# Transposed operands of a two-layer graph network: rearranging DMAs and 32x32 VectorE transposes with an HBM scratch, in place of TensorE transposes

## The chip, the cores and the metric

The kernel runs on one core of one Trainium2 chip. The metric is the device time of one execution in microseconds (us), on that core. "Clock" is the mean TensorE clock that the throttle granted, as a share of full speed. On one core there is no second die to compare with. The sessions ran on different chips; each ratio is to the kernel before in the same rounds on the same chip.

## The reference, cut to what matters

Batch 32, 512 nodes, 512 features, all fp32. Two layers, each with a LayerNorm without weights, a relu and a residual:

```python
h = max(layernorm(x), 0)
agg = (adj @ h) / max(rowsum(adj), 1e-6)
x = x + relu(concat(h, agg) @ W.T)                 # layer 0

h = max(layernorm(x), 0)
q, k = split(h @ Wqk);  v = h @ Wv
w = mask * rowdot(q, adj @ (mask * k)) / sqrt(512)
x = x + softmax(w, over nodes)[:, None] * v        # layer 1
```

Both kernels fold the weights so that one batch has five products of 512x512 matrices: y = h·W2, z = h·W1 + adj'·y (two products in one accumulator), q = h1·(Wq Wkᵀ), g = adj'·h1, and v = h1·Wv. adj' is the adjacency divided by the degree; layer 1 multiplies w by the degree again. A 512x512 product is done by Strassen's scheme in its Winograd form: seven half-size products of sums of quarters instead of eight.

The products here sum over the partitions of both operands. The left operands h (hT), h1 (h1T) and adj' (aT) must therefore be there transposed. The change is about how that happens.

## The kernel before

Each left operand is transposed by TensorE in 128x128 blocks into PSUM, the memory that TensorE writes its results to, and ScalarE evicts (copies out) four blocks at a time:

```python
def transpose_rows(dst, src, c, name):
    p = ps_t.tile([P, 2, 2, P], F32, tag="t", name=name)
    for d in range(4):
        nc.tensor.transpose(p[:, d // 2, d % 2, :], src(d), ident)
    half, m = divmod(c, 2)
    nc.scalar.activation(dst[:, 2 * half:2 * half + 2, :, ts(m, P)], p, AF.Copy)

def prepare(b):
    h0 = tile4(big, "h0", 1, f"h0_{b}")
    layer_norm(b, f"0_{b}", lambda c: h0[:, c, :])
    HT[b] = operand(big, "hT", 1, f"hT_{b}")
    for c in range(C):
        transpose_rows(HT[b], lambda d: h0[:, c, ts(d, P)], c, f"pth_{b}_{c}")
    left_sums(nc.vector, HT[b])
    # ... degree by a row sum, adjacency scaled by 1/degree on ScalarE ...
    for c in range(C):
        transpose_rows(AT[b], lambda d: an[:, c, ts(d, P)], c, f"pta_{b}_{c}")
    left_sums(nc.gpsimd, AT[b])
```

A product evicts three partial sums (r1, u2, u3) with ScalarE and ends its quarters on VectorE (mostly an add, and for z and v a "finish" into x). In the profiles, u3v is the sum u3 of product v, and av, bv and cv are v's three PSUM banks. The sixth of the seven groups of a product can't start before u3 is evicted, because it goes into the same PSUM bank. The batches are laid over one another in this order:

```python
for i in range(B):
    layer0_out(i)                # z of batch i
    if i > 0:
        layer1_out(i - 1)        # v of the batch before, output written
    if i + 1 < B:
        prepare(i + 1)           # LayerNorm 0's result and adjacency, transposed
        layer0_y(i + 1)          # y of the next batch
    layer1_h(i)                  # LayerNorm 1, h1T
    layer1_w(i)                  # q, g, softmax weights
    # ... cut: load(i + 2)
```

A scheduler fixes the order of every engine's queue at compile time, by its own estimate of when each instruction will be ready. An instruction that was written earlier may therefore come out later.

Of the kernel before, what the change touches and what calls it, by code (L numbers as in the profile page):

```python
# [10 lines left out]
F32 = mybir.dt.float32  # L11
# [4 lines left out]
P = 128  # L16
H = 256
# [5 lines left out]
def kernel(  # L23
# [23 lines left out]

    nc = tc.nc
# [9 lines left out]
    small = ctx.enter_context(tc.tile_pool(name="small", bufs=3))  # L58
    ps_t = ctx.enter_context(tc.tile_pool(name="ps_t", bufs=2, space=bass.MemoryType.PSUM))
# [26 lines left out]
    X, A = {}, {}  # L86

    def load(b):
        X[b] = tile4(big, "x", 3, f"x_{b}")
        nc.sync.dma_start(out=X[b], in_=x[b].rearrange("(c p) f -> p c f", p=P))  # L90
        A[b] = tile4(big, "adj", 1, f"adj_{b}")
        nc.sync.dma_start(out=A[b], in_=adj[b].rearrange("(c p) j -> p c j", p=P))

    def transpose_rows(dst, src, c, name):

        p = ps_t.tile([P, 2, 2, P], F32, tag="t", name=name)
        for d in range(4):
            nc.tensor.transpose(p[:, d // 2, d % 2, :], src(d), ident)  # L98
        half, m = divmod(c, 2)
        nc.scalar.activation(dst[:, 2 * half:2 * half + 2, :, ts(m, P)], p, AF.Copy)  # L100
# [55 lines left out]
    mask_sb = const.tile([B, N], F32, name="mask_sb")  # L156
    nc.sync.dma_start(out=mask_sb, in_=nodemask)
    w_in = []
    for half, tag in ((w0[:, F:2 * F], "x"), (w0[:, 0:F], "x"), (wqk[:, 0:F], "q"), (wqk[:, F:2 * F], "aT")):
        t = tile4(big, tag, {"x": 3, "q": 1, "aT": 2}[tag], f"w_in{len(w_in)}")  # L160
        nc.sync.dma_start(out=t, in_=half.rearrange("(c p) f -> p c f", p=P))
        w_in.append(t)
    w1, w2, wm, wvv = (operand(const, n, 1, n) for n in ("w1", "w2", "wm", "wvv"))
    for d in range(D):
        kh, kt = divmod(d, 2)
        nc.sync.dma_start(
            out=wvv[:, 2 * kh:2 * kh + 2, kt, :], in_=wv[ts(d, P), :].rearrange("p (n f) -> p n f", n=2)
        )
# [4 lines left out]
    HT, AT, Y, DEG = {}, {}, {}, {}  # L173
# [16 lines left out]
    def prepare(b):  # L190
        h0 = tile4(big, "h0", 1, f"h0_{b}")
        layer_norm(b, f"0_{b}", lambda c: h0[:, c, :])
        HT[b] = operand(big, "hT", 1, f"hT_{b}")
        for c in range(C):
            transpose_rows(HT[b], lambda d: h0[:, c, ts(d, P)], c, f"pth_{b}_{c}")
        left_sums(nc.vector, HT[b])

        deg = small.tile([P, C], F32, tag="deg", name=f"deg_{b}")
        rdeg = small.tile([P, C], F32, tag="rdeg", name=f"rdeg_{b}")
        nc.vector.tensor_reduce(deg, A[b], AX.X, ALU.add)  # L200
        nc.vector.tensor_scalar(deg, deg, DEG_EPS, None, op0=ALU.max)
        nc.vector.reciprocal(rdeg, deg)
        DEG[b] = deg
        an = A.pop(b)
        for c in range(C):
            nc.scalar.activation(an[:, c, :], an[:, c, :], AF.Copy, scale=rdeg[:, c:c + 1])
        AT[b] = operand(big, "aT", 2, f"aT_{b}")
        for c in range(C):
            transpose_rows(AT[b], lambda d: an[:, c, ts(d, P)], c, f"pta_{b}_{c}")
        left_sums(nc.gpsimd, AT[b])  # L210
# [21 lines left out]
    def layer1_h(b):  # L232

        h1 = H1[b] = operand(big, "h1", 1, f"h1_{b}")

        def rows(c):
            half, kt = divmod(c, 2)
            return h1[:, 2 * half:2 * half + 2, kt, :]

        layer_norm(b, f"1_{b}", rows)  # L240
        H1T[b] = operand(big, "h1T", 1, f"h1T_{b}")
        for c in range(C):
            half, kt = divmod(c, 2)
            transpose_rows(H1T[b], lambda d: h1[:, 2 * half + d // 2, kt, ts(d % 2, P)], c, f"pt1_{b}_{c}")
        left_sums(nc.vector, H1T[b])
        for c in range(C):
            nc.gpsimd.tensor_scalar(rows(c), rows(c), mraw[:, c, b:b + 1], None, op0=ALU.mult)  # L247
        right_sums(nc.gpsimd, h1)
# [55 lines left out]
    def layer1_out(b):  # L304
# [15 lines left out]
        nc.sync.dma_start(out=out[b].rearrange("(c p) f -> p c f", p=P), in_=xo)  # L320
# [3 lines left out]
    for c in range(C):  # L324
        nc.tensor.transpose(pmk[:, c, :], mask_sb[:, ts(c, P)], ident[:B, :B])
# [3 lines left out]
    for t, dst in zip(w_in[:2], (w2, w1)):  # L329
        for c in range(4):  # L330
            nh, m = divmod(c, 2)
            for kh in range(2):
                p = ps_t.tile([P, 2, P], F32, tag="t", name=f"ptw_{dst.name}_{c}_{kh}")
                for kt in range(2):
                    nc.tensor.transpose(p[:, kt, :], t[:, c, ts(2 * kh + kt, P)], ident)
                nc.scalar.activation(dst[:, 2 * kh + nh, :, ts(m, P)], p, AF.Copy)
        right_sums(nc.vector, dst)
    layer0_y(0)
    wT = []
    for t, tag in zip(w_in[2:], ("h1T", "h1")):  # L340
        dst = tile4(big, tag, 1, f"wT{tag}")
        for c in range(4):
            p = ps_t.tile([P, 4, P], F32, tag="t", name=f"ptk_{tag}_{c}")
            for d in range(4):
                nc.tensor.transpose(p[:, d, :], t[:, c, ts(d, P)], ident)
            nc.scalar.activation(dst[:, :, ts(c, P)], p, AF.Copy)
# [55 lines left out]
```

## Time and profile before

| | before |
|---|---|
| time, median of 4 runs | 2677.74 us (2677.62 to 2677.89) |
| TensorE busy | 97%, 12548 matmuls |
| granted clock | 0.999 |
| moved by DMA | 107.94 MB (after: 242.13 MB) |

Where are the transposes? The next lines are TensorE's timeline, with start, length, engine, line, operation, and the idle time before it in brackets. T0 is the end of z in the batch that is read; here it is 1059.97 us.

```profile
1067.56 1.04 PE L98 MATMUL pth<-ident,h 128*128 128x128 f32 x8
1069.98 1.99 PE L115 MATMUL av<-wvv,h1T 128*128 128x256 f32 x8 [1.38 <-ACT u3v L134]
1071.82 1.89 PE L115 MATMUL bv<-wvv,h1T 128*128 128x256 f32 x8
1073.54 1.04 PE L98 MATMUL pth<-ident,h 128*128 128x128 f32 x8
1074.42 0.60 PE L115 MATMUL ay<-w,hT 128*128 128x256 f32 x2
```

The first eight transposes of h fall into the time in which v waits for u3v's eviction. y starts 0.9 us after the last eight have begun, at T0+14.4. Hardly anything waits.

### The profile page before, as it was taken

What the parts mean: (1) busy time and instruction counts of PE and PEld (TensorE: products, weight loads), DVE (VectorE), ACT (ScalarE), POOL (GpSimd) and SP (SyncE); (2) the same over time, 40 slices, a digit from 0 to 9 for tenths busy, and PEclk for the clock granted to TensorE, in tenths of its full rate; (3) what the DMA queues carried; (4) which work ended last, traced back from release to release, by engine and by line L of the source; (5) the groups of instructions that cost most, each with busy time, mean ns of one, the idle gap of its engine ahead of it and who ended that gap; (6) DMA issues with size and microseconds to landing.
All of it is one profiled execution on the core that took longest, in us unless ns stands there. A gap on an engine that the chain in (4) does not pass through costs nothing.

```text
span 2677.8 us, 30643 instructions
## 1 busy us (share of the span) xinstructions
PE 2588.8 (97%) x12548; PEld 2208.7 (82%) x12548; DVE 1182.8 (44%) x2666; ACT 804.0 (30%) x1375; POOL 790.0 (30%) x590
## 2 busy tenths in 40 slices
PE   7999999999999999999999999999999999999998
PEld 4888888888888888888888888888888888888887
DVE  3443444444444444444433545344544444443434
ACT  4332233322233322233222333223332223332221
POOL 3322233312333212333123332223331233322231
PEclk9999999999999999999999999999999999999999
DMA  4011011110111110111101111101111011111000
GB/s 158 16 47 42 7 48 48 48 48 9 40 48 48 48 48 1 48 48 48 48 1 48 48 48 48 35 13 48 48 48 48 6 43 48 48 48 38 10 17 32
DMA packets 54076, 107.94 MB, mean 40 GB/s; under 512 B 1680, under 2 KB 2704, under 8 KB 53936
## 3 DMA queue, kind: packets, MB, share of 16 engines
q1 hardware_dynamic: 53936, 105.98, 11.3%
q8 instruction: 99, 1.62, 0.2%
q14 instruction: 41, 0.34, 0.0%
HBM read 72.42 MB, written 33.55 MB: 40 GB/s over the span
## 4 chain that ended last, share of the span: by engine, by line
PE 72%; DVE 14%; DMA 6%; ACT 5%; POOL 2%; issue 1%; DVEq 0%
PE az L115 17%; PE ag L115 9%; PE bz L115 8%; PE aq L115 7%; DVE st L182 5%; PE cz L115 4%; PE bg L115 4%; PE bq L115 4%; DMA adj<-in_adj_dram 4%; PE av L115 4%; PE ay L115 3%; ACT h L188 3%; PE bv L115 2%; POOL rstd L185 2%; PE cg L115 2%; PE pta L98 2%
## 5 line engine op out<-in xcount | busy, mean ns | idle before, releaser
L185 POOL TENSOR_TENSOR rstd<-rstd,mhalf 128x4 f32<-128x4 f32 x64 | 66.3, 1036 | 1374.6 <-DVE rstd L184 1366.4
L115 PE MATMUL av<-wvv,h1T 128*128 128x256 f32 x1024 | 250.7, 382 | 42.8 <-ACT u3v L134 42.8
L115 PE MATMUL az<-w,hT 128*128 128x256 f32 x1024 | 265.7, 382 | 0.3 <-ACT u3z L134 0.3
L115 PE MATMUL aq<-wm,h1T 128*128 128x256 f32 x1024 | 252.4, 384 | 13.6 <-DVE h1T L76 13.6
L115 PE MATMUL az<-y,aT 128*128 128x256 f32 x1024 | 262.8, 379 | 0.0
L115 PE MATMUL ay<-w,hT 128*128 128x256 f32 x1024 | 256.1, 383 | 2.5 <-ACT u3y L134 1.5
L115 PEld LDWEIGHTS av<-wvv,h1T 128*128 128x128 f32 x1024 | 191.8, 190 | 75.3 <-ACT u3v L134 50.6
L115 PE MATMUL ag<-h,aT 128*128 128x256 f32 x1024 | 249.5, 381 | 0.0
L247 POOL TENSOR_SCALAR h<-h,mraw 128x512 f32<-128x512 f32 x128 | 214.8, 1684 | 86.7 <-PE pt L98 86.7
L115 PEld LDWEIGHTS aq<-wm,h1T 128*128 128x128 f32 x1024 | 184.4, 190 | 50.7 <-ACT r1q L127 19.9
L188 ACT ACTIVATE h<-x,nb,rstd 128x512 f32<-128x512 f32 x256 | 196.7, 806 | 97.7 <-DVE nb L186 90.2
L115 PEld LDWEIGHTS ag<-h,aT 128*128 128x128 f32 x1024 | 191.9, 190 | 35.8 <-issue 11.0
L115 PEld LDWEIGHTS az<-w,hT 128*128 128x128 f32 x1024 | 191.9, 190 | 32.7 <-ACT u3z L134 7.5
L115 PEld LDWEIGHTS az<-y,aT 128*128 128x128 f32 x1024 | 194.6, 190 | 26.5
L115 PEld LDWEIGHTS ay<-w,hT 128*128 128x128 f32 x1024 | 184.3, 190 | 29.9 <-ACT u3y L134 10.1
L182 DVE BATCH_NORM_STATS2 st<-x 128x6 f32<-128x512 f32 x256 | 165.2, 677 | 8.0 <-DMA x<-in_x_dram 6.9
L225 DVE TENSOR_TENSOR u3z<-bz,u3z 128x512 f32<-128x512 f32 x32 | 22.1, 692 | 306.2 <-ACT u3z L134 306.2
L75 POOL TENSOR_TENSOR aT<-aT 128x512 f32<-128x512 f32 x32 | 40.6, 1269 | 367.3 <-ACT aT L100 367.3
L115 PE MATMUL bz<-y,aT 128*128 128x256 f32 x512 | 131.4, 379 | 0.0
L115 PE MATMUL bz<-w,hT 128*128 128x256 f32 x512 | 131.4, 379 | 0.0
L115 PE MATMUL by<-w,hT 128*128 128x256 f32 x512 | 123.4, 384 | 6.1 <-DVE y L144 6.1
L115 PE MATMUL bv<-wvv,h1T 128*128 128x256 f32 x512 | 121.2, 379 | 0.0
(155 smaller groups left out, 4155.1 us busy)
## 6 DMA issues: line engine op xcount, KB each, us to landing
x<-in_x_dram SPq DMA_DIRECT2D x32, 1024.0 KB, 5.8
adj<-in_adj_dram SPq DMA_DIRECT2D x32, 1024.0 KB, 6.1
out_dram<-x SPq DMA_DIRECT2D x32, 1024.0 KB, 5.0
w_in<-in_L_gnn_W_dram SPq DMA_DIRECT2D x2, 1024.0 KB, 10.6
w_in<-in_L_gnn_Wqk_dram SPq DMA_DIRECT2D x2, 1024.0 KB, 14.1
wvv<-in_L_gnn_Wv_dram SPq DMA_DIRECT2D x4, 256.0 KB, 10.0
mask_sb<-in_nodemask_dram SPq DMA_DIRECT2D x1, 64.0 KB, 7.8
```

Source lines behind the costliest of these rows:

```text
L75: eng.tensor_tensor(t[:, S1], t[:, S3], t[:, A22], op=ALU.add)
L98: nc.tensor.transpose(p[:, d // 2, d % 2, :], src(d), ident)
L115: nc.tensor.matmul(p[:, m, :], left[:, LEFT[k], kt, ts(m, P)], right[:, RIGHT[k], kt, :], start=(start and m == 0 and i == 0), stop=(i == ...
L182: nc.vector.bn_stats(st, X[b][:, c, :])
L185: nc.gpsimd.tensor_tensor(rstd, rstd, mhalf, op=ALU.pow)
L188: nc.scalar.activation(dst(c), X[b][:, c, :], AF.Relu, bias=nb[:, c:c + 1], scale=rstd[:, c:c + 1])
L225: nc.vector.tensor_tensor(u, p, u, op=ALU.add)
L247: nc.gpsimd.tensor_scalar(rows(c), rows(c), mraw[:, c, b:b + 1], None, op0=ALU.mult)
```

## The change

The intent is to take the transposes off TensorE, the engine that bounds the kernel. A DMA brings 32-row bands of the matrix to the four partition groups, and four VectorE instructions of 128x512 transpose all 32x32 blocks, from one half of the operand's tile into the other. x and adj come from HBM in that layout with no extra transfer. The LayerNorm results are in SBUF, so they are written to an HBM scratch and read back. The division by the degree is done on the staged adjacency by GpSimd. A matmul with a 0/1 matrix gives each partition the degrees that it needs. Core of the diff, weights and mask cut:

```diff
+    def transpose_staged(t, order):
+        v = staged(t).rearrange(f"p ({order}) (d a) -> p m l d a", m=4, d=4)
+        for m in range(4):
+            half, c = divmod(m, 2)
+            o = t[:, 2 * half:2 * half + 2, :, ts(c, P)].rearrange("p s k (l b) -> p l (s k) b", l=4)
+            nc.vector.transpose(o, v[:, m])
+    def through_hbm(name, chunk, t):
+        scr = dram.tile([N, F], F32, tag="scr", name=f"scr{name}")
+        for m in range(C):
+            nc.sync.dma_start(out=scr[ts(m, P), :], in_=chunk(m))
+        for q in range(4):
+            nc.sync.dma_start(
+                out=staged(t)[ts(q, Q)], in_=scr.rearrange("(r b) f -> b r f", b=Q)[:, :, ts(q, P)]
+            )
 ...
-        HT[b] = operand(big, "hT", 1, f"hT_{b}")
-        for c in range(C):
-            transpose_rows(HT[b], lambda d: h0[:, c, ts(d, P)], c, f"pth_{b}_{c}")
+        HT[b] = left("hT", 1, f"hT_{b}")
+        through_hbm(f"0_{b}", lambda m: h0[:, m, :], HT[b])
+        transpose_staged(HT[b], "m l")
         left_sums(nc.vector, HT[b])
 ...
+        nc.vector.tensor_reduce(part, staged(t), AX.X, ALU.add)
+        nc.tensor.matmul(pdeg, over_q.rearrange("p q b -> p (q b)"), part, start=True, stop=True)
+        nc.vector.tensor_scalar(degs, pdeg, DEG_EPS, None, op0=ALU.max)
+        nc.vector.reciprocal(part, degs)
+        nc.gpsimd.tensor_tensor(staged(t), staged(t), part.unsqueeze(2).to_broadcast([P, 16, P]), op=ALU.mult)
 ...
+        transpose_staged(t, "l m")
         left_sums(nc.gpsimd, t)
 ...   (layer 1: h1T likewise; its scaling by the mask moves from GpSimd to ScalarE)
```

More of the change, by code (lines that the diff above doesn't have):

```diff
@@ L16 @@
 P = 128
+Q = 32
 H = 256
@@ L58 @@
     small = ctx.enter_context(tc.tile_pool(name="small", bufs=3))
+    dram = ctx.enter_context(tc.tile_pool(name="dram", bufs=2, space=bass.MemoryType.DRAM))
     ps_t = ctx.enter_context(tc.tile_pool(name="ps_t", bufs=2, space=bass.MemoryType.PSUM))
@@ L84, in right_sums, with left, staged, rows_of @@
         eng.tensor_tensor(t[:, NT4], t[:, B21], t[:, T2], op=ALU.subtract)
-    X, A = {}, {}
+    X, AT = {}, {}
+    def left(tag, bufs, name):
+        return big.tile([P, 8, 2, H], F32, tag=tag, bufs=bufs, name=name)
+    def staged(t):
+        return t[:, 4:8].rearrange("p s k c -> p (s k c)").rearrange("p (r j) -> p r j", j=P)
+    def rows_of(t):
+        return [t[ts(l, P), :].rearrange("(m b) f -> b m f", b=Q) for l in range(4)]
+    def cols_of(t):
+        v = t.rearrange("p (q d a) -> p d q a", q=4, d=4)
+        return [v[:, d] for d in range(4)]
     def load(b):
         X[b] = tile4(big, "x", 3, f"x_{b}")
-        nc.sync.dma_start(out=X[b], in_=x[b].rearrange("(c p) f -> p c f", p=P))
-        A[b] = tile4(big, "adj", 1, f"adj_{b}")
-        nc.sync.dma_start(out=A[b], in_=adj[b].rearrange("(c p) j -> p c j", p=P))
-    def transpose_rows(dst, src, c, name):
-        p = ps_t.tile([P, 2, 2, P], F32, tag="t", name=name)
-        for d in range(4):
-            nc.tensor.transpose(p[:, d // 2, d % 2, :], src(d), ident)
-        half, m = divmod(c, 2)
-        nc.scalar.activation(dst[:, 2 * half:2 * half + 2, :, ts(m, P)], p, AF.Copy)
+        for l, r in enumerate(rows_of(x[b])):
+            nc.sync.dma_start(out=X[b][ts(l, Q)], in_=r)
+        AT[b] = left("aT", 2, f"aT_{b}")
+        for q in range(4):
+            nc.sync.dma_start(
+                out=staged(AT[b])[ts(q, Q)], in_=adj[b].rearrange("(r b) j -> b r j", b=Q)[:, :, ts(q, P)]
+            )
[9 more added lines that the diff above has]
+            nc.sync.dma_start(out=scr[ts(m, P), :], in_=chunk(m))
+        for q in range(4):
+            nc.sync.dma_start(
+                out=staged(t)[ts(q, Q)], in_=scr.rearrange("(r b) f -> b r f", b=Q)[:, :, ts(q, P)]
+            )
     def bank(name):
@@ L155 @@
     load(0)
-    mask_sb = const.tile([B, N], F32, name="mask_sb")
-    nc.sync.dma_start(out=mask_sb, in_=nodemask)
+    mask_sb = big.tile([B, C, P], F32, tag="h1", name="mask_sb")
+    for m, cols in enumerate(cols_of(nodemask)):
+        nc.sync.dma_start(out=mask_sb[:, m, :].rearrange("p (q a) -> p q a", q=4), in_=cols)
+    by_quad = const.tile([P, Q], F32, name="by_quad")
+    nc.vector.tensor_reduce(by_quad, ident.rearrange("p (q b) -> p b q", q=4), AX.X, ALU.add)
+    over_q = const.tile([P, 4, Q], F32, name="over_q")
+    for q in range(4):
+        nc.vector.tensor_copy(over_q[:, q, :], by_quad)
+    own_q = const.tile([P, 4], F32, name="own_q")
+    nc.vector.tensor_reduce(own_q, ident.rearrange("p (q b) -> p q b", q=4), AX.X, ALU.add)
     w_in = []
     for half, tag in ((w0[:, F:2 * F], "x"), (w0[:, 0:F], "x"), (wqk[:, 0:F], "q"), (wqk[:, F:2 * F], "aT")):
-        t = tile4(big, tag, {"x": 3, "q": 1, "aT": 2}[tag], f"w_in{len(w_in)}")
-        nc.sync.dma_start(out=t, in_=half.rearrange("(c p) f -> p c f", p=P))
+        t = big.tile([P, 16, 4, Q], F32, tag=tag, bufs={"x": 3, "q": 1, "aT": 2}[tag], name=f"w_in{len(w_in)}")
+        for q in range(4):
+            nc.sync.dma_start(
+                out=t[ts(q, Q)].rearrange("p r d a -> p r (d a)"),
+                in_=half.rearrange("(r b) f -> b r f", b=Q)[:, :, ts(q, P)],
+            )
         w_in.append(t)
@@ L166 @@
         nc.sync.dma_start(
-            out=wvv[:, 2 * kh:2 * kh + 2, kt, :], in_=wv[ts(d, P), :].rearrange("p (n f) -> p n f", n=2)
+            out=wvv[:, 2 * kh:2 * kh + 2, kt, :],
+            in_=wv.rearrange("(q d a) f -> d q a f", q=4, d=4)[d],
         )
@@ L171 @@
     mraw = const.tile([P, C, B], F32, name="mraw")
-    HT, AT, Y, DEG = {}, {}, {}, {}
+    HT, Y, DEG = {}, {}, {}
     def layer_norm(b, name, dst):
@@ L192, in prepare @@
         layer_norm(b, f"0_{b}", lambda c: h0[:, c, :])
-        HT[b] = operand(big, "hT", 1, f"hT_{b}")
-        for c in range(C):
-            transpose_rows(HT[b], lambda d: h0[:, c, ts(d, P)], c, f"pth_{b}_{c}")
+        HT[b] = left("hT", 1, f"hT_{b}")
+        through_hbm(f"0_{b}", lambda m: h0[:, m, :], HT[b])
+        transpose_staged(HT[b], "m l")
         left_sums(nc.vector, HT[b])
-        deg = small.tile([P, C], F32, tag="deg", name=f"deg_{b}")
-        rdeg = small.tile([P, C], F32, tag="rdeg", name=f"rdeg_{b}")
-        nc.vector.tensor_reduce(deg, A[b], AX.X, ALU.add)
-        nc.vector.tensor_scalar(deg, deg, DEG_EPS, None, op0=ALU.max)
-        nc.vector.reciprocal(rdeg, deg)
-        DEG[b] = deg
-        an = A.pop(b)
-        for c in range(C):
-            nc.scalar.activation(an[:, c, :], an[:, c, :], AF.Copy, scale=rdeg[:, c:c + 1])
-        AT[b] = operand(big, "aT", 2, f"aT_{b}")
-        for c in range(C):
-            transpose_rows(AT[b], lambda d: an[:, c, ts(d, P)], c, f"pta_{b}_{c}")
-        left_sums(nc.gpsimd, AT[b])
+        t = AT[b]
+        part = small.tile([P, 16], F32, tag="part", name=f"part_{b}")
+        nc.vector.tensor_reduce(part, staged(t), AX.X, ALU.add)
+        pdeg = ps_t.tile([P, 16], F32, tag="t", name=f"pdeg_{b}")
+        nc.tensor.matmul(pdeg, over_q.rearrange("p q b -> p (q b)"), part, start=True, stop=True)
+        degs = small.tile([P, 16], F32, tag="degs", name=f"degs_{b}")
+        nc.vector.tensor_scalar(degs, pdeg, DEG_EPS, None, op0=ALU.max)
+        nc.vector.reciprocal(part, degs)
+        nc.gpsimd.tensor_tensor(staged(t), staged(t), part.unsqueeze(2).to_broadcast([P, 16, P]), op=ALU.mult)
+        dl = degs.rearrange("p (l m) -> p l m", l=4)
+        nc.vector.tensor_tensor(dl, dl, own_q.unsqueeze(2).to_broadcast([P, 4, 4]), op=ALU.mult)
+        deg = DEG[b] = small.tile([P, C], F32, tag="deg", name=f"deg_{b}")
+        nc.vector.tensor_reduce(deg, degs.rearrange("p (l m) -> p m l", l=4), AX.X, ALU.add)
+        transpose_staged(t, "l m")
+        left_sums(nc.gpsimd, t)
     def layer0_y(b):
@@ L240, in layer1_h @@
         layer_norm(b, f"1_{b}", rows)
-        H1T[b] = operand(big, "h1T", 1, f"h1T_{b}")
-        for c in range(C):
-            half, kt = divmod(c, 2)
-            transpose_rows(H1T[b], lambda d: h1[:, 2 * half + d // 2, kt, ts(d % 2, P)], c, f"pt1_{b}_{c}")
+        H1T[b] = left("h1T", 1, f"h1T_{b}")
+        through_hbm(f"1_{b}", rows, H1T[b])
+        transpose_staged(H1T[b], "m l")
         left_sums(nc.vector, H1T[b])
         for c in range(C):
-            nc.gpsimd.tensor_scalar(rows(c), rows(c), mraw[:, c, b:b + 1], None, op0=ALU.mult)
+            nc.scalar.activation(rows(c), rows(c), AF.Copy, scale=mraw[:, c, b:b + 1])
         right_sums(nc.gpsimd, h1)
@@ L319, in layer1_out @@
         product(f"v_{b}", [(H1T.pop(b), wvv)], lambda p: finish(1, 0, p), rest)
-        nc.sync.dma_start(out=out[b].rearrange("(c p) f -> p c f", p=P), in_=xo)
+        for l, r in enumerate(rows_of(out[b])):
+            nc.sync.dma_start(out=r, in_=xo[ts(l, Q)])
     pmk = ps_t.tile([P, C, B], F32, tag="t", name="pmk")
     for c in range(C):
-        nc.tensor.transpose(pmk[:, c, :], mask_sb[:, ts(c, P)], ident[:B, :B])
+        nc.tensor.transpose(pmk[:, c, :], mask_sb[:, c, :], ident[:B, :B])
     nc.scalar.activation(mcol, pmk, AF.Copy, scale=scale)
@@ L329 @@
     for t, dst in zip(w_in[:2], (w2, w1)):
-        for c in range(4):
-            nh, m = divmod(c, 2)
-            for kh in range(2):
-                p = ps_t.tile([P, 2, P], F32, tag="t", name=f"ptw_{dst.name}_{c}_{kh}")
-                for kt in range(2):
-                    nc.tensor.transpose(p[:, kt, :], t[:, c, ts(2 * kh + kt, P)], ident)
-                nc.scalar.activation(dst[:, 2 * kh + nh, :, ts(m, P)], p, AF.Copy)
+        for d in range(D):
+            kh, kt = divmod(d, 2)
+            for nh in range(2):
+                nc.vector.transpose(
+                    dst[:, 2 * kh + nh, kt, :].rearrange("p (r b) -> p r b", b=Q), t[:, ts(nh, 8), d, :]
+                )
         right_sums(nc.vector, dst)
@@ L341 @@
         dst = tile4(big, tag, 1, f"wT{tag}")
-        for c in range(4):
-            p = ps_t.tile([P, 4, P], F32, tag="t", name=f"ptk_{tag}_{c}")
-            for d in range(4):
-                nc.tensor.transpose(p[:, d, :], t[:, c, ts(d, P)], ident)
-            nc.scalar.activation(dst[:, :, ts(c, P)], p, AF.Copy)
+        for d in range(D):
+            order = "p (d q b) -> p q d b" if tag == "h1T" else "p (q d b) -> p q d b"
+            nc.vector.transpose(
+                dst[:, d, :].rearrange(order, q=4, d=4), t[:, :, d, :].rearrange("p (q e) a -> p q e a", q=4)
+            )
         wT.append(dst)
```

## The prediction

> **What bounds the kernel now.** I read the head of the page first, then the TensorE groups by shape, then TensorE's waits, and last the timeline of one steady batch around its end of product z.
>
> ```profile
> span 2677.8 us, 30643 instructions
> PE 2588.8 (97%) x12548; PEld 2208.7 (82%) x12548; DVE 1182.8 (44%) x2666; ACT 804.0 (30%) x1375; POOL 790.0 (30%) x590
> ...
> L98 PE MATMUL pt<-ident,h 128*128 128x128 f32 x512 | 73.5, 276 | 2.3 <-ACT h L188 1.1 <-ACT h1T L100 1.1
> L98 PE MATMUL pta<-ident,adj 128*128 128x128 f32 x512 | 71.1, 282 | 1.4 <-ACT aT L100 1.0 <-ACT adj L206 0.3
> L98 PE MATMUL pth<-ident,h 128*128 128x128 f32 x512 | 68.7, 278 | 2.4 <-ACT h L188 1.2 <-ACT hT L100 0.8 <-ACT wTh L346 0.4
> ...
> PE av L115 <- ACT u3v L134: 42.8, 32, 1.4
> PE aq L115 <- DVE h1T L76: 13.6, 20, 1.0
> ```
>
> TensorE is the bound: busy 97%, with small waits. The r1z add of VectorE first starts at 70.6 us and last at 2598.9 us, 31 intervals, so one batch takes 81.56 us. Its 168 products of 128x128x256 are two matmuls each; a run of eight in the timeline advances by 1.727 us, so a product costs 0.4318 us and the batch 72.5 us. The other 9 us are 48 transposes, the wait of av (42.8/32 = 1.3 us) and small things. A batch goes z, v of the batch before, y of the next, q, g. Every transpose therefore lies on the bound; the groups give (73.5 + 71.1 + 68.7)/32 = 6.7 us a batch, of which the pipelined pitch (eight in 0.9 us) makes 48 x 0.11 = 5.3 us real.
>
> The second view is VectorE, ScalarE and GpSimd just after z has ended (T0 = 1059.97 us):
>
> ```profile
> 1065.71 0.17 DVE L184 TENSOR_SCALAR rstd<-mv 128x4 f32<-128x4 f32 x1
> 1067.03 0.16 DVE L186 SCALAR_TENSOR_TENSOR nb<-mv,rstd 128x4 f32<-128x4 f32 x1 [1.15 <-POOL rstd L185]
> ...
> 1067.23 2.22 ACT L188 ACTIVATE h<-x,nb,rstd 128x512 f32<-128x512 f32 x3 [2.32 <-DVE nb L186]
> 1069.36 0.57 ACT L134 ACTIVATE u3v<-av 128x512 f32<-128x512 f32 x1
> ...
> 1069.98 1.99 PE L115 MATMUL av<-wvv,h1T 128*128 128x256 f32 x8 [1.38 <-ACT u3v L134]
> ...
> 1095.45 1.75 DVE L78 TENSOR_TENSOR h1T<-h1T 128x512 f32<-128x512 f32 x1
> ...
> 1095.23 1.42 POOL L81 TENSOR_TENSOR y<-y 128x512 f32<-128x512 f32 x1
> ```
>
> The reader is to see three things: LayerNorm of layer 1 is ready at T0+7.2; the third eviction of v queues behind three LayerNorm activations, so v's last 16 matmuls start at T0+10.0; and a VectorE add that takes 0.69 us alone takes 1.75 us where a GpSimd add runs beside it.
>
> **What the skill says.** "VectorE: DVE Perf Modes", section "The three transpose paths": VectorE transposes 32x32 blocks only, 128x128 bf16 in 311 ns. For fp32 no run here shows it; I take a 128x512 transpose as any one-input pass of that size, 0.69 us (the rows of L75). "GPSIMD Engine Reference", section "Performance versus the Vector engine": a two-input GpSimd op of 2048 elements took 4497 ns. The trace has 512 elements at 1.27 us, 1.23 us from start to start, so four times that is 4.9 us; the two agree roughly. "SBUF — State Buffer", section "SBUF: two separate sides": a VectorE op with two SBUF inputs and a GpSimd op exclude each other for the whole instruction. The trace agrees: the 1.75 us above is a wait to the end of L81 plus 0.6 us. "DMA: Bandwidth & Descriptors", section "Anatomy of one DMA": a DMA has about 2 us of fixed cost; here 1 MB lands in 5.8 us.
>
> **The change, part by part, per batch of 81.56 us.**
> Removed from TensorE: 48 transposes, 5.3 us. Removed from ScalarE: 12 evictions of 0.59 us and 4 scalings of 0.72 us, 9.9 us, against 4 activations of 0.8 us added. Off TensorE's path these are worth little. If nothing else happened, a batch would be 72.5 + 0.9 (four tiny matmuls and switches) + at least 0.6 for u3v = 74 us: 2440 us in all.
> Added to VectorE: 12 transposes x 0.69 = 8.3 us on 37 us; it stays near 55% busy, so throughput is not the matter, order is. Added to GpSimd: one multiply of the staged adjacency by 1/degree, 128x2048, 4.9 us, for 4 x 1.57 us taken away. Added DMA: two 1 MB writes and two 1 MB reads through HBM; 7 MB a batch in all instead of 3. At the measured 5.8 us per MB this is about 40 us of 80: hidden as throughput.
>
> The compiled order of the changed kernel decides the rest. VectorE is in order, and its queue after z reads: LayerNorm statistics, the degree operations (they wait for the degree matmul, which TensorE has after the fifth group of v), add and finish of u3v, aT transpose 1 (waits for the GpSimd multiply), finish of av, aT transpose 2, add of u2v, aT transpose 3, finish of u2v, then the four hT transposes, aT transpose 4, the hT sums. Product y needs hT. So y now waits for the adjacency of a later product. Walk, in us after T0:
> - degree matmul after 18 products of v: 18 x 0.4318 = 7.8, done 7.9; maximum and reciprocal (0.3 + 0.2): 8.4.
> - GpSimd multiply 4.9: 13.3.
> - u3v: evicted 10.0, added 10.7; its finish has two SBUF inputs, so it is held to 13.3; two finishes 0.88: 14.2.
> - three aT transposes 3 x 0.69, two finishes of two halves 1.76, one add 0.69, first hT transpose 0.69: 5.2, so y starts at 19.4.
> - v ended at about 10.0 + 16 x 0.216 = 13.5. TensorE idles 6 us.
> - y 28 x 0.4318 = 12.1, with 0.5 for sums that collide with GpSimd's: 32.0.
> - last add of y 0.7, then first h1T transpose 0.7 (behind it in the queue): q starts at 33.4, another 1.4 idle.
> - q needs S2 3.5 later; four transposes and two sums take 4.2, and GpSimd's y sums exclude them: about 1 us more.
> - q, g, z and the first of v, 114 x 0.4318 = 49.2, small 0.9.
> Sum 33.4 + 1 + 50.1 = 84.5 us, against 81.56: +2.9 us. Thirty-one batches: +91 us.
>
> Edges: the start loads weights in pieces, writes and reads h0 through HBM, and does 24 weight transposes on VectorE; y of batch 0 started at 22.8 us and I estimate about 15 us later. The last batch has no y to hide behind; its LayerNorm ends at T0+11.7, write and read are some 3 + 7 us, plus the wait of the output writes ahead: about 12 us more. Together +27 us. Total 2678 + 91 + 27 = 2796 us; I say 2800.
>
> **Rivals.**
> (a) The plain gain: the multiply is done early, hT is ready when v ends, 2440 to 2500 us. For it: TensorE is 97% busy and 5.3 us a batch is really taken off. Against it: the order above, in which the multiply cannot start before T0+8.4 and hT's transposes stand behind it.
> (b) The HBM round trip is the new wait. hT's read waits for z's last use of the buffer and is issued at T0-1; even 10 us land before 13. h1T's read is issued behind the output writes, which wait for the last finish of v (T0+18.7); with 8 issues of 0.4 us it lands near T0+29, 3 us before it is needed. If 512-byte rows cost twice what I take, q starts 4 us later: 2930 us.
> (c) fp32 transposes run at half rate (1.2 us). Four of them lie ahead of y, one to two ahead of q's first matmuls: +3 us a batch, 2890 us.
> (d) The finish of u3v isn't held and the multiply is shorter (4 us): y starts at 17.5; a batch is about 82 us, and only the edges show: 2710 us.
>
> **Range and chances.** The centre is the walk; (d) gives the low end, (b) and (c) the high end. Eight times in ten between 2690 and 2930 us. Slower by over 2% (above 2731 us): 0.74. Within 2%: 0.15. Faster by over 2%: 0.11, for (a) or for an order that the times of the chip make harmless.
>
> **What would show it.** TensorE's wait list should have ay waiting for the hT transpose in nearly all batches, some 6 us each, 190 us in all, and aq for the h1T transpose 1 to 3 us each; VectorE's aT transpose should wait for the GpSimd multiply; TensorE's busy share should fall below 90%. A transpose of 128x512 at 0.69 us and a multiply near 4.9 us confirm the terms. If ay waits for a DMA instead, (b) holds; if ay doesn't wait and the batch is near 74 us, the walk is wrong at the multiply.

## More of the kernel before

The softmax makes one small transpose a batch, `ptop`. Its row gives the distance between batches: it has the count, the durations, and the first and last start.

```profile
L286 PE MATMUL ptop<-ident,top x32: 272/273/273, 137.8 to 2660.3; 128*1 128x128 f32 x32
```

The first comes at 137.8 us, the last at 2660.3 us. The mean of the 31 distances is (2660.3 - 137.8)/31 = 81.37 us; this is the number used for every run below. (The last one is shorter, as no further batch is prepared in it. The 30 before it have a mean of 81.89 us.)

## The result, and the profile after

| | before | after |
|---|---|---|
| time, median of 4 runs | 2677.74 us | 2889.61 us (2882.42 to 2919.34) |
| ratio | | 1.0812, 95% interval 1.0737 to 1.0888 |
| mean distance of batches | 81.37 us | 86.83 us |
| granted clock, profiled run | 0.999 | 0.976 |

Ratios here and below are the mean time of one kernel's fast runs over that of the other's in the same rounds, so they aren't quite the ratio of the medians quoted. The four runs of after had clocks of 0.976, 0.950, 0.968 and 0.968 with times of 2882, 2919, 2888 and 2891 us: the lower the clock, the longer. The kernel before spread by 0.3 us.

First the head of the page, TensorE's list of waits (total us, times, longest) and the `ptop` row:

```profile
span 2880.6 us, 29494 instructions
PE 2488.5 (86%) x11012; PEld 2089.9 (73%) x11012; DVE 1594.7 (55%) x3144; ACT 609.1 (21%) x967; POOL 753.0 (26%) x494
...
PE ay L152 <- DVE hT L127: 172.7, 32, 43.6
PE av L152 <- ACT u3v L171: 66.3, 32, 2.5
PE aq L152 <- DVE h1T L127: 60.4, 32, 14.2
PE ag L152 <- ACT r1g L164: 22.1, 29, 0.8
...
PE ay L152 <- DVE hT L83: 7.5, 15, 0.5
...
L338 PE MATMUL ptop<-ident,top x32: 272/273/273, 169.7 to 2861.5; 128*1 128x128 f32 x32
```

TensorE is 100 us less busy than before, and the kernel is 203 us longer: over 300 us of idle time are new. y waits for the VectorE transpose of hT in each of the 32 batches. The only DMA in the list is one wait of 13.8 us for the mask at the start.

Where the 203 us (spans) lie: the first `ptop` comes 31.9 us later, 30 distances are longer by 5.10 us each (86.98 instead of 81.89), the last one by 16.3, and what follows the last by 1.7. That is 31.9 + 153 + 16.3 + 1.7.

Now the timeline of a batch with T0 = 1062.16 us, all engines, cut to the chain:

```profile
1061.32 1.90 SPq L135 DMA_DIRECT2D hT<-scr  x4
...
1070.68 3.61 POOL L257 TENSOR_TENSOR aT<-aT,part 128x2048 f32<-128x2048 f32 x1 [1.52 <-DVE part L256]
...
1072.86 3.13 DVE L362 SCALAR_TENSOR_TENSOR x<-u3v,sm,x 128x256 f32<-128x256 f32 x2
1073.98 1.89 PE L152 MATMUL bv<-wvv,h1T 128*128 128x256 f32 x8
1074.31 1.40 POOL L88 TENSOR_TENSOR h<-h 128x512 f32<-128x512 f32 x1
1075.91 0.70 DVE L127 STREAM_TRANSPOSE aT<-aT 128x512 f32<-128x512 f32 x1
...
1079.11 0.83 DVE L362 SCALAR_TENSOR_TENSOR x<-u2v,sm,x 128x256 f32<-128x256 f32 x2
1079.86 2.48 DVE L127 STREAM_TRANSPOSE hT<-hT 128x512 f32<-128x512 f32 x4
1080.70 3.23 PE L152 MATMUL ay<-w,hT 128*128 128x256 f32 x8 [4.83 <-DVE hT L127]
1083.73 2.36 PE L152 MATMUL cy<-w,hT 128*128 128x256 f32 x8
...
1097.16 1.97 PE L152 MATMUL aq<-wm,h1T 128*128 128x256 f32 x8 [1.49 <-DVE h1T L127]
```

Read it from the bottom. y's first group starts at 1080.70, 0.84 us after the four hT transposes began: it follows the first of them. Ahead of those, VectorE did the last finish of v; ahead of that, transposes of aT; ahead of that, u3v's two finishes, which took 3.13 us instead of 0.88. They ran beside two GpSimd instructions, the multiply (to 1070.68 + 3.61 = 1074.29) and the sum of h behind it (to 1074.31 + 1.40 = 1075.71), and ended 0.28 us after the second. Yet hT's read was issued at 1061.32, and such reads land 5.0 us after issue: the data lay there some ten microseconds before VectorE turned to it.

One more thing stands in the durations. Eight matmuls of `ay` take 3.23 us here, where 1.9 to 2.0 is normal: the granted clock in the trace is 0.50 from 1081.25 to 1084.66, after the idle time. In the batch before, the same happens earlier, from 985.67 to 989.09:

```profile
985.59 3.68 PE L152 MATMUL av<-wvv,h1T 128*128 128x256 f32 x8 [2.10 <-ACT u3v L171]
...
994.15 1.97 PE L152 MATMUL ay<-w,hT 128*128 128x256 f32 x8 [3.15 <-DVE hT L127]
...
998.77 1.97 PE L152 MATMUL ay<-w,hT 128*128 128x256 f32 x8 [0.50 <-DVE hT L83]
```

There `av` was slow after a wait of 2.10 us, v ended later, and y waited only 3.15 us. The two patterns alternate from batch to batch in this stretch. In both, y starts at T0+18.5. It ends at T0+33.5 where y's first group was slow, and at T0+32.6 where v's was; these batches take 87.50 and 86.55 us from one T0 to the next.

### The profile page after: what moved, and what is told of

Its sections match the earlier page's. It is cut to its first block, busy times and chain, and to the rows that moved or that the text cites. A ratio compares the mean times of both kernels' runs of the same rounds, so it can differ in the third digit from the quotient of the medians.

```text
span 2880.6 us, 29494 instructions
## 1 busy us (share of the span) xinstructions
PE 2488.5 (86%) x11012; PEld 2089.9 (73%) x11012; DVE 1594.7 (55%) x3144; ACT 609.1 (21%) x967; POOL 753.0 (26%) x494
## 2 busy tenths in 40 slices
DMA packets 303070, 242.13 MB, mean 84 GB/s; under 512 B 15184, under 2 KB 253776, under 8 KB 302928
## 4 chain that ended last, share of the span: by engine, by line
issue 50%; PE 25%; DVE 15%; ACT 4%; POOL 3%; SPq 1%; DMA 1%; DVEq 0%; POOLq 0%
PE ay L152 8%; PE aq L152 6%; DVE x L362 5%; PE by L152 4%; DVE st L233 3%; ACT h L239 2%; POOL rstd L236 2%; PE bq L152 2%; PE cq L152 2%; DVE hT L127 2%; DVE aT L127 2%; PE cy L152 1%; DVE hT L83 1%; DVE h1T L127 1%; DVE u3v L368 1%
## 5 line engine op out<-in xcount | busy, mean ns | idle before, releaser
L152 PE MATMUL ay<-w,hT 128*128 128x256 f32 x1024 | 273.5, 414 | 201.5 <-DVE hT L127 172.7
L152 PEld LDWEIGHTS ay<-w,hT 128*128 128x128 f32 x1024 | 202.1, 204 | 259.5 <-issue 143.6
L152 PE MATMUL av<-wvv,h1T 128*128 128x256 f32 x1024 | 275.7, 411 | 66.3 <-ACT u3v L171 66.3
L152 PEld LDWEIGHTS av<-wvv,h1T 128*128 128x128 f32 x1024 | 207.5, 206 | 100.5 <-ACT u3v L171 70.0
L152 PE MATMUL ag<-h,aT 128*128 128x256 f32 x1024 | 251.7, 383 | 22.4 <-ACT r1g L164 22.1
L278 DVE TENSOR_TENSOR u3z<-bz,u3z 128x512 f32<-128x512 f32 x32 | 22.1, 691 | 230.9 <-ACT u3z L171 230.9
L257 POOL TENSOR_TENSOR aT<-aT,part 128x2048 f32<-128x2048 f32 x32 | 115.5, 3609 | 63.6 <-DVE part L256 63.6
L152 PE MATMUL bq<-wm,h1T 128*128 128x256 f32 x512 | 120.9, 379 | 0.0
```

Source lines behind the costliest of these rows:

```text
L152: nc.tensor.matmul(p[:, m, :], left[:, LEFT[k], kt, ts(m, P)], right[:, RIGHT[k], kt, :], start=(start and m == 0 and i == 0), stop=(i == ...
L257: nc.gpsimd.tensor_tensor(staged(t), staged(t), part.unsqueeze(2).to_broadcast([P, 16, P]), op=ALU.mult)
L278: nc.vector.tensor_tensor(u, p, u, op=ALU.add)
```

## The experiments

The theory: y (and with it the batch) is set by the order of VectorE's queue. hT's transposes stand behind the aT transposes, which wait for the multiply, and behind v's finishes. The skill says that VectorE, ScalarE and GpSimd are strict FIFO (the Trainium skill, "Perfetto Trace Analysis", section "Tensor Engine Instruction (MATMUL, LD_WEIGHTS)"). The trace agrees: the transposes, whose data had landed by about T0+6, ran at T0+17.7, after everything listed before them. The rivals: the latency of the HBM round trip, the transposes' own time, and the slow clock. Each run had three rounds beside the kernel before; correctness was as it should be (one is wrong on purpose).

| run | median us | ratio to before, 95% interval | batch us | clock |
|---|---|---|---|---|
| before (medians of other sessions: 2676 to 2679) | 2677.7 | 1 | 81.37 | 0.999 |
| after | 2889.6 | 1.0812 (1.0737 to 1.0888) | 86.83 | 0.976 |
| no_trip | 2883.6 | 1.0771 (1.0755 to 1.0787) | 86.75 | 0.976 |
| early | 2935.2 | 1.0967 (1.0951 to 1.0984) | 88.51 | 0.942 |
| early3 | 2936.9 | 1.0973 (1.0955 to 1.0992) | 88.57 | 0.942 |
| h_only | 2948.7 | 1.1023 (1.1004 to 1.1041) | 88.95 | 0.968 |
| adj_only | 2658.9 | 0.9934 (0.9920 to 0.9949) | 80.57 | 0.997 |
| adj_early3 | 2678.0 | 1.0003 (0.9988 to 1.0018) | 81.34 | 0.991 |
| warm | 2879.2 | 1.0755 (1.0739 to 1.0771) | 86.70 | 0.991 |
| mult_dve | 2918.3 | 1.0901 (1.0853 to 1.0949) | 88.03 | 0.965 |
| ht_order | 2845.5 | 1.0629 (1.0611 to 1.0647) | 85.61 | 0.962 |
| ht_order2 | 2717.3 | 1.0153 (1.0138 to 1.0168) | 81.55 | 0.978 |
| ht_order4 | 2593.9 | 0.9688 (0.9672 to 0.9704) | 77.64 | 0.995 |
| before_u3v | 2644.5 | 0.9876 (0.9860 to 0.9893) | 80.25 | 0.998 |

### no_trip: is it the round trip?

```diff
-   in_=scr.rearrange("(r b) f -> b r f", b=Q)[:, :, ts(q, P)]
+   in_=x[b].rearrange("(r b) f -> b r f", b=Q)[:, :, ts(q, P)]     # wrong result on purpose; writes kept
```

> Wrong result on purpose: the two reads that should fetch the LayerNorm results back from the scratch read the input x of the same batch, with the same shape, so they no longer wait for the writes; the writes are still done, so the traffic is the same. Round-trip rival: the waits of y and q vanish, about 5 us per batch less, near 2720 us. Queue theory: a steady batch stays within 0.5 us of 87.0, and only the first and last batch gain, together 10 to 30 us: 2860 to 2885 us.

The batch stayed at 86.75 us: in the changed kernel's own order the round trip is hidden. The time, 2883.6 us, lies at the lower edge of after's own spread, so even the 10 to 30 us expected at the first and last batch didn't show. The first y still waited 43.1 us; I had charged part of that to the round trip, and the run doesn't support it. It doesn't clear the round trip at the start either: its reads still stand behind the writes in the DMA queue and were issued from 44.95 to 51.07 us, where after's were from 51.07 to 52.98. The section on the prediction says what that wait is.

### early: the adjacency out of the way

```diff
+    def prepare_adj(b):              # degree, multiply, transposes and sums of aT, split off from prepare
 ...
+        if i + 1 < B:
+            prepare_adj(i + 1)
         layer0_out(i)
```

> The adjacency's work (row sums, degree matmul, reciprocal, GpSimd multiply, four transposes, sums) is issued one product earlier, ahead of z, so that nothing of it stands ahead of the hT transposes in VectorE's queue or makes u3v's finish wait. Queue theory: y starts near T0+16 instead of T0+18.5, its wait falls from 3.2 to 4.8 us to about 2.4 us (v's own finishes still stand ahead of hT), the half-clock stretch gets shorter or goes; a batch takes about 83.5 us and the kernel about 2780 us. Rival, the HBM round trip's latency: nothing changes, 2880 to 2900 us. Rival, the transposes' own time: nothing changes either, as the same number is done.

It got slower by some 45 us. The step it aimed at came out as expected, y waits 2.42 us. But another wait grew. TensorE's lines of one batch:

```profile
1091.68 3.78 PE L152 MATMUL av<-wvv,h1T 128*128 128x256 f32 x8 [3.44 <-ACT u3v L171]
1095.26 3.07 PE L152 MATMUL bv<-wvv,h1T 128*128 128x256 f32 x8
1100.74 0.47 PE L152 MATMUL ay<-w,hT 128*128 128x256 f32 x1 [2.42 <-DVE hT L127]
```

The wait for u3v is 3.44 us instead of 2.10, and both groups of v after it run at about half rate. v ends so late that y, still queued behind v's finishes, starts at T0+20.2 instead of T0+18.5. In the trace GpSimd's sums of aT run beside VectorE's finish of r1v (2.04 us for the pair that takes 0.85 in after), the LayerNorm comes over a microsecond later, and ScalarE evicts u3v only after three LayerNorm activations. Moving the adjacency away was not enough, since v's finishes still stood ahead of hT.

### early3: the same with the sums later

```diff
-        left_sums(nc.gpsimd, t)                  # at the end of prepare_adj
+            left_sums(nc.gpsimd, AT[i + 1])      # after prepare(i + 1) in the main loop
```

> As the run 'early', which was slower than the change although y's own wait fell to 2.4 us: there the GpSimd sums of aT ran beside r1v's finish, the LayerNorm came 1.2 us later, u3v's wait grew to 3.4 us and both halves of v after it ran at half clock. Here those sums are issued after the LayerNorm. If that reading is right, u3v's wait is 1.4 to 2.1 us, y starts near T0+16, TensorE's busy time falls below 2500 us and the kernel takes 2780 to 2830 us. If it stays near 2930 us, the earlier multiply or transposes are to blame, not the sums.

It stayed at 2937 us, but this doesn't put the blame elsewhere: the scheduler moved the sums back to where they were, and in the trace they again ran beside r1v's finish. The run is a repetition of early and tests nothing new. The lesson is to check in the compiled order that an edit has arrived.

### adj_only and h_only: the two halves of the change

adj_only is the kernel before with the adjacency's part alone; h_only is the changed kernel with the adjacency back on TensorE.

```diff
 # adj_only, against the changed kernel
-        through_hbm(f"0_{b}", lambda m: h0[:, m, :], HT[b])
-        transpose_staged(HT[b], "m l")
+        for c in range(C):
+            transpose_rows(HT[b], lambda d: h0[:, c, ts(d, P)], c, f"pth_{b}_{c}")     # h1T likewise
 # h_only: the reverse, prepare's adjacency part as before, tmps with 6 buffers instead of 7 for room
```

> The kernel before with the adjacency's part of the change alone: rearranging DMA, VectorE transposes, staged multiply on GpSimd; both LayerNorm results are transposed by TensorE as before, no scratch. TensorE loses 16 of 48 transposes (1.8 us a batch), and no VectorE transpose stands ahead of y's or q's first operand. Queue theory: y no longer waits for VectorE; 79.5 to 80.5 us a batch, 2620 to 2660 us. If the GpSimd multiply's exclusion of u3v's finish is by itself the cost, u3v's wait stays at 2.1 us and the kernel is at 2680 us or above.

> The changed kernel with the adjacency transposed by TensorE as before; both LayerNorm results go through HBM and VectorE transposes. TensorE loses 32 of 48 transposes (3.5 us a batch). Queue theory: hT's transposes still stand behind v's finishes, but not behind the adjacency's; y starts near T0+16, its wait is about 2.5 us plus a short slow-clock stretch, 83 to 84 us a batch, about 2760 to 2780 us. Round-trip rival: as long as the change, 2880 us or above, since it keeps the whole round trip.

adj_only takes 2658.9 us, at the upper end of what was expected and 0.7% faster than before. So the rearranging DMA, the GpSimd multiply and four VectorE transposes don't hurt by themselves. h_only was a miss: 2948.7 us. Its wait at y fell as expected, to 1.45 us with y at T0+16.0, but q now waits for u3q, because the scheduler put all four activations of the next LayerNorm ahead of u3q's eviction on ScalarE:

```profile
1130.59 2.93 ACT L234 ACTIVATE h<-x,nb,rstd 128x512 f32<-128x512 f32 x4 [3.91 <-DVE nb L232]
1133.42 0.57 ACT L175 ACTIVATE u3q<-aq 128x512 f32<-128x512 f32 x1
...
1134.05 3.57 PE L156 MATMUL aq<-wm,h1T 128*128 128x256 f32 x8 [3.69 <-ACT u3q L175]
```

This is again a matter of queue order, on another engine, and again the matmuls after it are slow. So h_only doesn't say what the round trip costs.

### adj_early3

```diff
+        if i + 1 < B:
+            prepare_adj(i + 1)       # added to adj_only, ahead of layer0_out(i)
```

> adj_only (2659 us, the adjacency's part of the change alone) with the degree, the multiply and the transposes of the adjacency moved ahead of z, its sums left where they are. A batch of adj_only has waits of 1.4 us at u3v and 1.5 us at u3g; moving the multiply away should leave the first and may remove the second: 79 to 80.5 us per batch, 2600 to 2650 us, the best version if so. If u3v's wait grows beyond 2 us as in 'early', the clock falls and it is slower than 2680 us.

A miss: 2678 us, slower than adj_only by 19 us. u3v's waits grew from 42.0 us to 78.3 us in total, as in early.

### warm: is it the clock?

```diff
+    def keep_warm(i):
+        p = ps_t.tile([P, 2, H], F32, tag="t", name=f"warm_{i}")
+        for _ in range(9):
+            nc.tensor.matmul(p[:, 0, :], ident, w2[:, 0, 0, :], start=True, stop=True)
```

> The changed kernel with nine products of the identity with a weight tile added per batch, whose result nobody reads, placed where TensorE waits: three in the u3v wait, six between the end of v and y. Clock theory: a wait of 2 to 5 us costs more than itself, because the matmuls after it run at about half rate (8 matmuls in 3.2 to 3.8 us instead of 1.97); with the waits filled the granted clock goes from 0.968-0.976 to about 0.995 and 1.5 to 2 us per batch are gained, about 2830 us, though no operand comes earlier. Rival, the waits alone: the added work fills idle time only, so 2880 to 2890 us as before, or some us more.

The clock rose to 0.991, and the time hardly moved (2879.2 us, batch 86.70). This was the most useful miss. With TensorE at full rate, y's first two groups were done earlier, but the third needs a sum of hT quarters (the second one on VectorE). The mixed timeline of warm (T0 = 1059.64) shows it (the view names no releaser; the group starts 0.11 us after the sum's end):

```profile
1079.64 1.89 PE L152 MATMUL cy<-w,hT 128*128 128x256 f32 x8
...
1081.00 1.64 DVE L83 TENSOR_TENSOR hT<-hT 128x512 f32<-128x512 f32 x1
...
1082.75 1.97 PE L152 MATMUL ay<-w,hT 128*128 128x256 f32 x8 [1.22 <-issue]
```

The sum ends at 1082.64, T0+23.0; in after it ended at T0+23.0 too. So a part of the slow clock's cost in y was hidden under VectorE's queue, but not all of it. The run is no clean test of the rest: its compiled order differs too (hT's first transpose comes before v's last finish, and y's third group comes before two matmuls that precede it in after). After's own trace is the better witness: of its two patterns, the one with the slow group in y takes 0.95 us longer, so an estimate from these two is 0.5 us a batch, of the 5.10 to be explained. A slow group in v costs y nothing there. In the changed kernel the slow clock is mostly a consequence of the waits and a small cause; in early, where v itself was slowed ahead of the finishes, it did lie on the path.

### mult_dve: is it the multiply?

```diff
-        nc.gpsimd.tensor_tensor(staged(t), staged(t), part.unsqueeze(2).to_broadcast([P, 16, P]), op=ALU.mult)
+        nc.vector.tensor_tensor(staged(t), staged(t), part.unsqueeze(2).to_broadcast([P, 16, P]), op=ALU.mult)
```

> The changed kernel with the staged adjacency's multiply on VectorE instead of GpSimd. If the GpSimd multiply (3.6 us, holding u3v's finish and the aT transposes) is the term that delays y, y starts near T0+16.5 instead of T0+18.5 and its wait falls to about 2.5 to 3 us: 1.5 to 2 us per batch less, about 2830 us. If the place of the aT and hT transposes in VectorE's queue is all that counts, the multiply takes 2 to 2.5 us of the same queue and y starts where it does now: 2870 to 2890 us.

Slower than the change, 2918.3 us. y started at T0+18.9 in the batch read; over the steady batches it starts between T0+17.3 and T0+20.1, on average at 18.5 as in after, and y itself takes 1.2 us longer. The multiply took 2.29 us of VectorE's queue instead of 3.61 on GpSimd, but v's finishes came no earlier. The scheduler also interleaved the rest differently, so the run only says that moving the multiply off GpSimd doesn't bring the 5 us back.

### ht_order: the same instructions in another order

After these, one statement of the theory was left: it is the place of hT's transposes behind v's finishes as well. Here that place alone is changed by hand. `issue_after(i)` only fixes issue order on one engine, it adds no wait.

```diff
         layer0_out(i)
+        if i + 1 < B:
+            prepare(i + 1)                        # without the adjacency, which follows v
         if i > 0:
             layer1_out(i - 1)
 ...
+            with tc.issue_after(LAST[b + 2]):     # last hT transpose; here u3v's add, likewise av's finish
+                nc.vector.tensor_tensor(u, p, u, op=ALU.add)
 ...
+        with tc.issue_after(LAST[b]):
+            transpose_staged(t, "l m")            # the aT transposes
```

> The changed kernel with the same instructions, but VectorE's queue put in another order: the four hT transposes come right after the LayerNorm and degree operations, and v's last three finishes and the aT transposes stand behind them. In the changed kernel's trace hT's read was issued at T0-1 and should have landed near T0+5, while its first transpose ran at T0+17.7. Queue theory: y's wait for hT disappears (under 0.5 us), y starts near T0+13.7 instead of T0+18.5, and unless h1T's read or the sums become the next wait, q starts at T0+29 to T0+31 instead of T0+35: 81 to 83 us per batch, 2690 to 2760 us. Round-trip rival: hT isn't there at T0+8, VectorE stands still before the transpose waiting for a DMA, and it takes 2880 us or more. Clock rival: the clock rises with the wait gone, but as in 'warm' the time doesn't follow.

TensorE's list of waits:

```profile
PE aq L153 <- DVE h1T L127: 150.3, 32, 14.0
PE av L153 <- ACT u3v L172: 66.3, 32, 2.5
PE ay L153 <- DVE hT L127: 53.0, 2, 43.1
```

y's wait fell from 32 times to two, the first batch and the second. In the batch read, hT's transposes started at T0+8.8 with no DMA wait before them. That settles y: its wait was queue order, neither the round trip nor the transposes' time. The time fell by only 44 us, though, short of what I expected, because a new wait took the place: q for h1T, about 5 us in a batch where it had been 1.5. The DMA queue (SPq) of one batch (T0 = 1135.51) and what followed:

```profile
1150.54 0.84 SPq L136 DMA_DIRECT2D h1T<-scr  x2
1157.74 2.87 SPq L387 DMA_DIRECT2D out_dram<-x  x4
1160.65 2.42 SPq L136 DMA_DIRECT2D h1T<-scr  x2
...
1168.06 3.75 PE L153 MATMUL aq<-wm,h1T 128*128 128x256 f32 x8 [5.32 <-DVE h1T L127]
```

Two of the four reads of h1T stand behind the output writes, which wait for v's last finish, now later.

### ht_order2 and ht_order4: the next two queues

ht_order2 issues the output writes after h1T's reads. ht_order4 adds two more orders: u3v's eviction ahead of the LayerNorm activations, and h1T's transposes ahead of y's last add.

```diff
 # ht_order2
+        if i > 0:
+            store(i - 1, READ[i])        # output writes, with issue_after(last read of h1T)
 # ht_order4, in addition
+        with tc.issue_after(EV[f"v_{b - 1}"]):
+            layer_norm(b, f"1_{b}", rows)
+            with tc.issue_after(behind):          # behind: last h1T transpose; y's last add only
+                nc.vector.tensor_tensor(dst(half, nh), p, u, op=ALU.add)
```

> In 'ht_order' y no longer waits, but q now waits for h1T's transpose, mostly about 5 us, and its first matmuls then run at half clock: in the DMA queue the last two reads of h1T stand behind the four output writes, which wait for v's last finish. Here the output writes are issued after h1T's reads; nothing else is changed by hand. If that queue position is the reason, q's wait falls to about 1.5 us, its first groups run at full clock, and a batch falls from 85.6 to 81 to 83 us: 2690 to 2750 us. If the reads themselves are too slow, the wait stays and so does 2845 us.

> As 'ht_order2', with two more orders changed: ScalarE evicts u3v before the three LayerNorm activations, not after them (u3v's wait of 2.1 us should fall to about 0.7), and VectorE does h1T's transposes before y's last add (q's wait of 1.5 us should nearly go). Queue theory: another 2 to 3 us per batch less, 78.5 to 80.5 us, 2610 to 2690 us, at or below the kernel before. If the order isn't what holds it, it stays at the time of 'ht_order2'.

ht_order2 came to 2717.3 us; q waited 54.7 us in all instead of 150.3. ht_order4 came to 2593.9 us, below the lower end of what I expected. Head and waits of ht_order4:

```profile
span 2592.1 us, 29436 instructions
PE 2426.2 (94%) x11012; PEld 2060.5 (79%) x11012; DVE 1551.0 (60%) x3144; ACT 605.6 (23%) x967; POOL 754.2 (29%) x494
...
PE ay L154 <- DVE hT L127: 53.1, 2, 43.3
PE ay L154 <- ACT u3y L175: 21.3, 31, 0.7
PE av L154 <- ACT u3v L175: 18.2, 32, 0.7
...
PE aq L154 <- DVE h1T L127: 10.3, 1, 10.3
```

The counts of busy instructions on PE, DVE, ACT and POOL are those of the changed kernel to the last one, and so is the DMA volume (242.13 MB). Only the order differs, by 296 us. y now starts at T0+10.3 and q at T0+26.1, where after had 18.5 and, in its two patterns, 35.0 and 34.1.

### before_u3v: a control

ht_order4 has one improvement that the kernel before could have had too.

```diff
+        with tc.issue_after(EV[f"v_{b - 1}"]) if b > 0 else ExitStack():
             layer_norm(b, f"1_{b}", rows)
```

> A control for 'ht_order4' (2594 us): the kernel before with the one reordering of 'ht_order4' that applies to it too, u3v's eviction ahead of the LayerNorm activations on ScalarE. It takes away some 0.7 of the 1.4 us that v waits: 2640 to 2660 us, if the fuller ScalarE queue behind it delays nothing. If it comes near 2594 us, the gain of 'ht_order4' is not the removed transposes' but the eviction's; if it is 2640 us or above, the removed transposes, with the queues in order, are worth the rest.

2644.5 us, as expected. Against a kernel before with that order too, ht_order4 is still 1.9% faster (2593.9/2644.5, the medians of different rounds). No other order of the kernel before was tried. But TensorE is busy for 2592.0 of the 2643.5 us of before_u3v's profile, so an order without any idle time, the start included, would only reach the 2592.1 us of ht_order4's profile. So the removed transposes do pay, once the queues don't give the gain back. The best version is ht_order4, 3.1% faster than before.

## Why the prediction was right or wrong

The class (slower), the time within the range, and the mechanism (y behind VectorE's queue) were right. The centre was 90 us low. By its own steps, with T0 as in the timeline of after (a second number is of the other pattern):

- *Degree matmul 7.9, reciprocal 8.4*: measured 7.9 and 8.4.
- *GpSimd multiply 4.9, from four times a 512-element add*: 3.61 us. It ended at T0+12.1, not 13.3. Scaling a short op by its size overstated it.
- *u3v's finish held*: right, 3.13 us for the pair; it ended at T0+13.8 (predicted 14.2). That this came so close is partly luck: the multiply was 1.2 us earlier than walked, but GpSimd's next sum, which the walk doesn't have, held the pair on, so that it ended 1.7 us after the multiply and not 0.9. The aT transposes, which were to wait for the multiply, waited for it once, 3.3 us at the start; after that the finish ahead of them had done the waiting.
- *Transposes 0.69 each*: measured 0.66 to 0.70; rival (c) falls.
- *y starts at 19.4, after 6 us of idle*: 18.5, after 4.83 or 3.15 us.
- *y takes 12.1 + 0.5*: the step that failed most. It took 15.0 us (T0+18.5 to T0+33.5), or 14.0. In the timeline 1.3 us more lie in the slow first group, 0.5 in the second, and 0.7 in a wait for u3y. In the other pattern y's matmuls run at full rate; there the third group waits 0.50 us for VectorE's second sum of hT, and the wait for u3y is the same. So three terms were missing or too small: u3y's eviction (21.3 us in 31 waits), VectorE's work after the first transpose (three more of hT, one of aT, sums held by GpSimd), and the slow clock in every second batch.
- *q starts at 33.4*: 35.0 or 34.1, with 1.49 us wait where 1.4 was said.
- *The rest, 51.1*: 52.5 in both patterns (87.50 - 35.0 and 86.55 - 34.1). Of this, 0.8 us is a wait of g for the eviction of r1g (22.1 us in 29 waits), which the walk doesn't have.
- *Edges +27*: +50 (31.9 + 16.3 + 1.7), mostly the first batch. There the reason is the DMA queue: h0 was ready on ScalarE at 15.2 us, but its first write to the scratch was issued at 38.05, behind 20 reads of weights, the reads back at 51.07, when the writes had landed, and hT's first transpose started at 59.17. So by the trace 22.8 us of this are the queue's order and 21.1 the round trip; no run changed either.

So 2.5 us a batch (84.5 against 86.98), about 1.1 of it before q's start and 1.4 after it, and 23 us of edges were missing. The rivals: (a), the plain gain, was called unlikely for this order, and rightly; the experiments show that it was the order and not the work that denied it, although even the best order measured reached 2594, not 2440 to 2500. (b), the round trip, falls for the steady batch of the changed kernel (no_trip), but its concern about reads queued behind the output writes became real in ht_order as soon as y stopped waiting. (d) was half right (a shorter multiply, but the finish was held).

One implication of the walk fell. It reads as though the multiply and the aT transposes were the cause: take them away and the batch gets shorter. In h_only y did start earlier without them, at T0+16.0. In early it started later, since v ended later, and in mult_dve, which only moved the multiply, on average where it did before. None of the three was faster. The finishes of v alone are enough to hold hT (y still waits 1.45 us in h_only and 2.42 in early), and among these runs y was free only when both stood behind it.

What stays open: how much of the start could be won by another order of its DMA queue, as no run changed it; how much of a batch is left in the remaining short waits; and the size of the clock's own part in early, as no run filled its gaps.

## What to carry to other kernels

Work that is moved to an idle engine joins an in-order queue; before counting the gain, find what stands ahead of it there, on the engine and on the DMA queue, and compare the time the data lands with the time the instruction runs. When a change that takes work off the bound is slower, try the same instructions in another order before giving it up: here that was worth 296 us, more than the change had cost. After each such fix look for the next wait, and check in the compiled order that the edit has arrived.

## What the Trainium skill lacked or had wrong

- "TensorE: Matmul & The Clock Gate", section "Why this matters for your kernels", asks for no idle gaps over about 3 us between matmul bursts. Here a gap of 2.10 us was followed by a slow group in some batches (8 matmuls in 3.68 us, with the clock at 0.50 from 985.67 to 989.09) and not in others (1.99 us). So a gap under 3 us wasn't always safe.
- "GPSIMD Engine Reference", section "Performance versus the Vector engine": 4497 ns for a two-input op of 2048 fp32 elements. The multiply here, whose second input is broadcast from 16 values, took 3609 ns on average. That section has no figure for a broadcast input.
- "VectorE: DVE Perf Modes", section "The three transpose paths", has a figure for bf16 only. A 128x512 fp32 transpose of 32x32 blocks took 0.67 to 0.69 us on average, as long as the LayerNorm statistics' pass over 128x512 (0.68 us). The same section warns of plain DMAs that do a transpose by strides, where the innermost stride of the destination is large. Here they only rearrange, in runs of 512 bytes, which the section doesn't treat: 256 KB landed in about 5 us, four at a time, hidden in the steady batch.
